# A slot-attention and FP8 feed-forward kernel: first loads reordered, one group of transposes and three split steps moved

## The chip, the cores and the metric

The kernel runs on one core of a Trainium2 chip. The metric is the device time of one execution in microseconds, as the median of several runs. A core has five engines that each work through a queue of their own in order: PE (TensorE), DVE (VectorE), ACT (ScalarE), POOL (GpSimd) and SP, which here issues most of the DMAs.

## The reference

Four sequences of 512 tokens with 512 channels pass through one layer: a gated slot attention with 16 heads (64 key channels, 64 slots, 128 value channels), then a feed-forward block whose weights are rounded to FP8.

```python
x = x + attn(layernorm(x), Wq, Wk, Wv, Wg, Ws, Wo, g_norm_weight)
x = x + ffn(layernorm(x), gate_w, up_w, down_w, gate_scale, up_scale, down_scale)

# attn, per head:
s = clip(h @ Ws, -32, 32); z = cumlogsumexp(s)      # over time
g = exp(z_before - z);     p = exp(s - z)
hk = hk * g + k p^T;       ok = (q * scale) hk       # first recurrence
hv = hv * g + p v^T;       ov = softmax(ok) hv       # second recurrence
o  = ov * rsqrt(mean(ov^2) + eps) * g_norm_weight * silu(h @ Wg)
return o @ Wo
# ffn:
return ((silu((h @ q(gate_w)) * gate_scale) * (h @ q(up_w)) * up_scale) @ q(down_w)) * down_scale
```

## The kernel before, in words

**Units.** Heads are taken in pairs (8 groups `g`), and a unit is one pair of heads for one sequence `b`. Sequences 0 and 1 go through all groups first, then 2 and 3; unit 0 is (0, 0), unit 1 is (0, 1). A sequence has 4 blocks of 128 tokens (`NT`), and 512 channels are 4 chunks (`KC`).

**Order.** The scheduling is manual: every engine executes its instructions in the order in which the Python code issues them. `first_unit` writes out unit 0 by hand, and `attention` writes out every later unit. Steps that are not tied to a place wait in two lists: `steps` holds the transposes of a later sequence's norm blocks (`next_step()` takes one), and `work` holds VectorE and ScalarE steps, mostly the splitting of weights. `other(n)` takes n entries of `work`, without a number as many as `pace[0]` says (2 in unit 1); `piece()` takes entries until one of them was a full step; `need(key)` takes entries until none with that name is left.

**Split operands.** Products of 32-bit precision are made from three float32r products: an operand is split into a high part (ScalarE, times `UNDER`), a low part and a third part (VectorE). For a norm block, `transposes(n)` turns the block with four TensorE transposes into a PSUM bank and ScalarE writes the high part (L358); `parts(n)` has VectorE write the low and the third part (L368, L370). The low part is then multiplied by 1/`DELTA` in place on ScalarE (`scale_low`, L310), one block later than its split, and after the last block through an entry of `work` of its own. For a weight matrix, `load_matrix` puts an entry `high(0)` (named with a trailing `_`) and one `step(n)` for each 512 columns into `work`: a step has ScalarE write the next high half (L253) and VectorE the two other parts (L260, or L262 for Wq, and L265). After the last step, SP writes the split matrix to DRAM (L273); steps of Wo also call `fetch()` for the next raw weights (L210).

**Sequence 0** is different: its first products use the unsplit values (`xn_whole`, and raw weights), and its split follows later.

**PSUM.** `bank()` hands out three banks in turn (scores, transposes, states); a product that gets a bank must wait until the reader of its last content is done. Projections (`proj`) have three buffers, and so the first write into one waits for the reader of a former projection.

**The start.** SP's queue loads block 0 of sequence 0, the two halves of Wv for the first pair of groups (`raw_v`, 512 KB each), blocks 1 to 3, then raw Ws, Wk, Wq, sequence 1 and raw Wg; the latter lands in the place that the split Wo takes later (tag `w_o`). In the norm of sequence 0, VectorE measures a block (L339 to L341), POOL takes a power (L342), VectorE normalises (L346), TensorE transposes (L353), ScalarE copies (L356). The measuring of block n + 1 is issued ahead of the normalising of block n. The values of block 0 (`values(0)`, L565) come between the transposes of blocks 0 and 1.

**The tail of unit 0 and unit 1.** After the gates and the softmax come the weights' transposes (ps_w, then wT at L758), `weight_slot` (ps_b at L611, masked on VectorE at L615), `read_out` (ps_ov at L772 and L781), then unit 1 with `slots` (ps_s, eT), `keys` (with `running_sum`, the scan z at L677, in between), `queries`, the transposes ps_e and ps_kn, `values(0)`, `values(1)`.

Of the kernel before, what the change touches and what calls it, by code (L numbers as in the profile page):

```python
# [44 lines left out]
P = 128  # L45
# [4 lines left out]
def kernel(  # L50
# [18 lines left out]
    nc = tc.nc  # L69
# [7 lines left out]
    KC = D // P  # L77
# [32 lines left out]
    def bank(name, n=None):  # L110
        if n is None:
            n = turn[0]
            turn[0] = (n + 1) % 3
        if n in held:
            held.pop(n)()
        return ps1.tile([P, 512], F32, tag=f"bank{n}", name=name)
# [50 lines left out]
    def other(count=None):  # L167
        for _ in range(count or pace[0]):
            if work:
                work.pop(0)[1]()  # L170

    def piece():

        while work:
            name, run = work.pop(0)
            run()
            if not name.endswith("_") and run is not scale_low:
                break

    def need(key):  # L180

        while any(name == key for name, _ in work):
            other(1)
# [4 lines left out]
    for g in range(NG):  # L188
# [3 lines left out]
        for nm in names:  # L192
            n = g if nm != "v" else 0 if g == 0 else (g + 1) // 2
# [5 lines left out]
    def fetch():  # L199
        if to_fetch:  # L200
            nm, g, part, chunks = to_fetch.pop(0)
            src, width = MATRICES[nm]
            tag = f"raw{fetched[0] % 2}"
            fetched[0] += 1
            w = one.tile([P, RAW], F32, tag=tag, name=f"raw_{nm}_{g}_{part}")[:, : chunks * width]
            if nm == "o":
                rows = src[g * HV : (g + 1) * HV, :]
            else:
                rows = src[part * chunks * P : (part + 1) * chunks * P, g * width : (g + 1) * width]
            nc.sync.dma_start(  # L210
                w.rearrange("p (c n) -> p c n", c=chunks), rows.rearrange("(c p) n -> p c n", p=P)
            )
            raw.setdefault((nm, g), []).append(w)
# [72 lines left out]
    def turned():  # L286

        return bool(work) and work[0][0][:3] == "xs_"

    def next_step():  # L290
        if steps:
            steps.pop(0)()
# [21 lines left out]
    whole = []  # L314

    def layernorm(b, which, n_bank=None, first=None):
# [33 lines left out]
        def transposes(n):  # L350
            pt = bank(f"ps_xn{which}_{b}_{n}", n_bank).rearrange("p (c t) -> p c t", c=KC)
            for c in range(KC):
                nc.tensor.transpose(pt[:, c, :], xn[n][:, c * P : (c + 1) * P], ident)  # L353
            hi = dst[0][:, :, n * P : (n + 1) * P]
            if start:
                nc.scalar.copy(whole[0][:, :, n * P : (n + 1) * P], pt)  # L356
            elif which == 1:
                nc.scalar.mul(hi, pt, UNDER)  # L358
            else:
                nc.scalar.copy(hi, pt)  # L360
            pts[n] = pt
# [513 lines left out]
    def exp_and_log():  # L875
        nc.scalar.preload_act_table_set("natural_log_exp_and_others")

    def first_unit():


        X = Heads(0, 0)

        parts = layernorm(0, 1, first=lambda: X.values(0))
        for nm in "skqv":
            load_matrix(nm, 0, True)
        for item in [item for item in work if item[0] in ("s_", "k_", "q_")]:
            work.remove(item)
            item[1]()
        X.values(1)
        for _ in range(5):  # L890
            piece()
        transposing = layernorm(1, 1)
        work.extend(parts())
        load_matrix("g", 0, True)
        other(2)
        X.slots()
        other(2)
        X.keys(X.running_sum)
        other(2)
        X.queries(None)  # L900
        X.turn_e()
        X.turn_k()
        other(2)
        X.values(2)
        other(2)
        X.key_states()
        X.inverse()
        X.values(3)
        fetch()
        fetch()  # L910
        load_matrix("o", 0, True)
        other(1)
        transposing()
        next_step()
        other(2)
        X.query_key()
        next_step()
        other(3)
        X.gate_main(0)
        X.slot_scores()  # L920
        X.value_states()
        next_step()
        next_step()
        X.softmax()
        X.softmax_exp()
        other(1)
        X.gate_main(1)
        X.slot_weights()
        other(1)
        X.gate_silu(0)  # L930
        X.gate_silu(1)
        exp_and_log()
        X.weight_slot()
        X.softmax_sum()
        need("xs_0")
        piece()
        piece()
        X.read_out()
        return X

    def attention(g, b, before, load, gated):

        X = Heads(g, b)
        even = g % 2 == 0
        small = other if even or b > 1 or pace[0] > 1 else piece
        first = pace[0] > 1 and even and b == 1

        def early_step():  # L950

            if not any(name.endswith("_m") for name, _ in work):
                next_step()

        need(f"xs_{b}")
        need("s")
        X.slots()
        load("s")
        if not even:
            early_step()  # L960
        before.scale_output()
        need("k")

        def running_sum():
            before.scale_other()
            X.running_sum()
            if first:
                other(1)
            else:
                small()  # L970

        X.keys(running_sum)
        load("k")
        if not even:
            early_step()
        need("q")
        X.queries(other if even or turned() else None)
        load("q")
        X.turn_e()
        if even:  # L980
            X.turn_k()
            next_step()
            if turned():
                other(1)
            need("v")
            X.values(0)
            X.values(1)
            before.turn_output(0)
            before.high_output(0)
            before.turn_output(1)  # L990
            before.high_output(1)
            X.key_states()
            X.inverse()
            X.query_key()
            other()
            X.values(2)
            before.split_output(0)
            next_step()
            other()
            X.values(3)  # L1000
            other()
            next_step()
            before.split_output(1)
        else:
            before.turn_output(0)
            X.turn_k()
            before.turn_output(1)
            before.high_output(0)
            before.high_output(1)
            X.query_key()  # L1010
            X.key_states()
            before.split_output(0)
            before.split_output(1)
            X.inverse()
            if work and work[0][1] is scale_low:
                other(1)
            if work and work[0][0] == "o":
                other()
        need("g")
        X.gate_main(0)  # L1020
        before.low_output(0)
        before.low_output(1)
        X.gate_mixed(0)
        if even:
            other()
            next_step()
        elif work and work[0][0] == "o":
            other()
        X.gate_main(1)
        X.gate_mixed(1)  # L1030
        load("g")
        if even:
            load("v")
        gated()
        X.gate_silu(0)
        X.gate_silu(1)
        exp_and_log()
        X.slot_scores()
        X.value_states()
        X.softmax()  # L1040
        if not turned():
            small()
        need("o")
        before.project_output(0)
        X.softmax_exp()
        before.add_output(0)
        before.project_output(1)
        X.slot_weights()
        before.add_output(1)
        next_step()  # L1050
        before.project_output(2, True)
        before.add_output(2)
        small()
        before.project_output(3)
        load("o")
        X.weight_slot()
        before.add_output(3)
        X.softmax_sum()
        if even or b > 1 or steps:
            other()  # L1060
        next_step()
        if turned():
            other(1)
        X.read_out()
        return X
# [81 lines left out]
    with tc.manual_schedule(engines=EVERY):  # L1147
        blocks = x[0].rearrange("(n p) d -> p n d", p=P)
        x1[0] = two.tile([P, NT, D], F32, tag="v", name="x1_0")
        for n in range(NT):  # L1150
            nc.sync.dma_start(x1[0][:, n, :], blocks[:, n, :])
            if n == 0:
                fetch()
                fetch()
        exp_and_log()
        fetch_first()
# [155 lines left out]
```

## Time and profile before

| | |
|---|---|
| median of 3 runs | 1462.33 us (1461.22 to 1462.84) |
| the profiled execution | 1460.5 us, of which 1458.8 us are the span of its instructions |
| TensorE busy | 1433.3 us (98%) |
| VectorE busy | 1101.6 us (76%) |
| ScalarE busy | 713.1 us (49%) |
| mean granted TensorE clock | 0.999 |
| unit 0 | until about 55 us |
| unit 1 | from there to about 98 us |

Times in the profile count from the first instruction. In a line of the timeline the first number is the start and the second the length, both in us; the bracket at the end is the idle time of the engine just before, and what ended it. PE matmul records may stand for several products that follow each other; a 32-bit product has two records and a float32r product one.

### The profile page before, as it was taken

The page shows a single profiled execution, that of the slowest core. Times are in us where ns is not written, and L with a number is a line of the kernel's source. Part 1 is how long each engine was busy: PE and PEld are TensorE (multiplying, and loading weights), DVE is VectorE, ACT ScalarE, POOL GpSimd, SP SyncE. Part 2 cuts the span into 40 slices and gives each one's busy share as a digit, 9 for nine tenths or more (in the row PEclk, how much of TensorE's full clock was granted, in tenths as well). Part 3 has the DMA queues.
Part 4 walks back from the last instruction along what each step waited for, and adds up shares of the span by engine and source line. Part 5 has one row for each costly group of instructions (what it writes and reads, how often), then busy time and mean ns, then how long its engine had stood idle before and what let it go on. Part 6 is the DMA issues. An engine that isn't in the chain of part 4 may idle for free.

```text
span 1458.8 us, 23013 instructions
## 1 busy us (share of the span) xinstructions
PE 1433.3 (98%) x9067; PEld 1171.4 (80%) x9067; DVE 1101.6 (76%) x1966; ACT 713.1 (49%) x1214; POOL 197.7 (14%) x206
## 2 busy tenths in 40 slices
PE   8999999999999999999999999999999999999998
PEld 4788888888888887888888888888888888888886
DVE  7788768876887689878888888898888874445333
ACT  4665555655564556454544564456345643222221
POOL 2011111111111111211111111111112120000000
PEclk9999999999999999999999999999999999999999
DMA  8275456564656464456546654666455562101000
GB/s 335 108 207 174 138 151 174 174 217 130 174 173 208 110 231 123 138 159 188 164 111 187 202 173 96 194 202 174 123 181 174 148 178 29 58 0 59 0 29 29
DMA packets 80715, 212.52 MB, mean 146 GB/s; under 512 B 6152, under 2 KB 34848, under 8 KB 75424
## 3 DMA queue, kind: packets, MB, share of 16 engines
q1 hardware_dynamic: 62080, 177.49, 32.8%
q0 software_dynamic: 18528, 33.58, 15.9%
q8 instruction: 71, 1.16, 0.3%
q14 instruction: 36, 0.29, 0.1%
HBM read 107.23 MB, written 108.00 MB: 148 GB/s over the span
## 4 chain that ended last, share of the span: by engine, by line
PE 82%; DVE 11%; issue 4%; ACT 2%; DMA 0%; POOL 0%; SPq 0%; DVEq 0%; ACTq 0%; POOLq 0%
PE ps_o L857 8%; PE ps_g L517 7%; PE ps_v L576 7%; PE ps_fg L1073 6%; PE ps_fu L1073 6%; PE ps_o_m L857 4%; PE ps_g_m L540 4%; PE ps_v_m L576 4%; PE ps_ov L781 4%; PE ps_s L517 3%; PE ps_q L517 3%; PE ps_k L517 3%; PE ps_fd L1122 3%; PE ps_fe L1122 2%; PE ps_b L611 2%
## 5 line engine op out<-in xcount | busy, mean ns | idle before, releaser
L873 POOL DMA_DIRECT2D stream<-y x128 | 112.9, 890 | 826.8 <-DVE y L872 819.7
L857 PE MATMUL ps_o<-w_o,oT 128*128 128x512 f32 x512 | 144.1, 403 | 0.0
L517 PE MATMUL ps_g<-xs,w_g 128*128 128x512 f32 x496 | 125.2, 394 | 0.0
L576 PE MATMUL ps_v<-w_v,xs 128*128 128x512 f32 x480 | 122.4, 397 | 0.3 <-ACT v L584 0.3
L1094 DVE SCALAR_TENSOR_TENSOR h<-ps_fu,scol,act 128x512 f32<-128x512 f32 x48 | 36.0, 750 | 105.9 <-PE ps_fu L1073 104.6
L867 ACT ACTIVATE y<-ps_o 128x512 f32<-128x512 f32 x128 | 76.6, 599 | 76.2 <-PE ps_o L857 73.4
L517 PEld LDWEIGHTS ps_g<-xs,w_g 128*128 128x128 f32 x496 | 91.7, 188 | 19.8
L857 PEld LDWEIGHTS ps_o<-w_o,oT 128*128 128x128 f32 x512 | 91.5, 188 | 16.8
L576 PEld LDWEIGHTS ps_v<-w_v,xs 128*128 128x128 f32 x480 | 87.7, 188 | 19.6 <-ACT v L584 0.8
L1073 PE MATMUL ps_fg<-xs,wf 128*128 128x512 f32 x384 | 96.5, 393 | 0.0
L1073 PE MATMUL ps_fu<-xs,wf 128*128 128x512 f32 x384 | 95.0, 389 | 0.0
L872 DVE TENSOR_TENSOR y<-y,ps_o_m 128x512 f32<-128x512 f32 x128 | 87.1, 680 | 9.7 <-ACT y L867 8.9
L584 ACT ACTIVATE v<-ps_v 128x512 f32<-128x512 f32 x60 | 36.0, 599 | 99.5 <-PE ps_v L576 99.5
L1073 PEld LDWEIGHTS ps_fu<-xs,wf 128*128 128x128 f32 x384 | 72.1, 188 | 15.2
L791 ACT ACTIVATE og<-ps_ov 128x512 f32<-128x512 f32 x64 | 38.1, 597 | 93.4 <-PE ps_ov L781 93.4
L1073 PEld LDWEIGHTS ps_fg<-xs,wf 128*128 128x128 f32 x384 | 71.1, 188 | 14.4
L585 DVE TENSOR_TENSOR v<-v,ps_v_m 128x512 f32<-128x512 f32 x60 | 41.0, 684 | 53.7 <-PE ps_v_m L576 53.7
L857 PE MATMUL ps_o_m<-w_o,oT 128*128 128x512 f32 x256 | 79.2, 391 | 0.1
L1100 ACT CAST both<-h 128x512 fp32r<-128x512 f32 x48 | 29.8, 621 | 96.8 <-DVE h L1094 96.8
L522 ACT ACTIVATE sg<-ps_g 128x512 f32<-128x512 f32 x62 | 37.2, 599 | 72.7 <-PE ps_g L517 58.0
L1091 ACT ACTIVATE act<-ps_fg,scol 128x512 f32<-128x512 f32 x48 | 33.0, 688 | 80.9 <-PE ps_fg L1073 80.9
L796 POOL TENSOR_TENSOR rs<-rs,mhalf 128x8 f32<-128x8 f32 x32 | 58.8, 1839 | 89.7 <-DVE rs L793 76.4
(169 smaller groups left out, 3260.8 us busy)
## 6 DMA issues: line engine op xcount, KB each, us to landing
stream<-y POOLq DMA_DIRECT2D x128, 256.0 KB, 5.9
split_v<-w_v SPq DMA_DIRECT2D x4, 3072.0 KB, 14.6
split_g<-w_g SPq DMA_DIRECT2D x8, 1536.0 KB, 6.8
split_o<-w_o SPq DMA_DIRECT2D x8, 1536.0 KB, 6.2
w_v<-split_v SPq DMA_DIRECT2D x4, 3072.0 KB, 15.4
w_g<-split_g SPq DMA_DIRECT2D x8, 1536.0 KB, 6.5
w_o<-split_o SPq DMA_DIRECT2D x8, 1536.0 KB, 9.4
rounded<-qw SPq DMA_DIRECT2D x36, 256.0 KB, 3.4
```

Source lines behind the costliest of these rows:

```text
L517: nc.tensor.matmul(self.p, products(self.nm, c, self.col0, i), xs[self.b][i][:, c, :], start=(i == 0 and c == 0), stop=(i == 1 and c == KC ...
L540: nc.tensor.matmul(self.m, products(self.nm, c, self.col0, 2), xs[self.b][2][:, c, :], start=(c == 0), stop=(c == KC - 1),)
L576: nc.tensor.matmul(dst, xs[b][i][:, c, n * P : (n + 1) * P], wt["v"][:, i, c * 2 * HV : (c + 1) * 2 * HV], start=(i == which[0] and c == 0 ...
L585: nc.vector.tensor_tensor(to, to, m, ALU.subtract)
L781: nc.tensor.matmul(po[h][:, n, :], self.bb[h][:, n, :], both_v[self.b][:, n, self.v0 + h * DV : self.v0 + (h + 1) * DV], start=False, stop ...
L796: nc.gpsimd.tensor_tensor(rs, rs, mhalf.rearrange("p (h n) -> p h n", h=HG), ALU.pow)
L857: nc.tensor.matmul(dst, self.oT[:, i, h, n * P : (n + 1) * P], wt["o"][:, i, h * D : (h + 1) * D], start=(i == which[0] and h == 0), stop= ...
L867: nc.scalar.mul(y, p, 1.0 + DELTA)
L872: nc.vector.tensor_tensor(y, y, m, ALU.subtract)
L873: nc.gpsimd.dma_start(stream[self.b][n * P : (n + 1) * P, :], y, accum_op=ALU.add)
L1073: nc.tensor.matmul(pp, w[:, c * P : (c + 1) * P], xs[b][k][:, c, :], start=(c == 0 and k == 0), stop=(c == KC - 1 and k == 1),)
L1122: nc.tensor.matmul(sums[n], parts[k][:, n * P : (n + 1) * P], fw[c][2], start=(c == 0 and k == 0), stop=(c == NFC - 1 and k == 1),)
```

## The change

Four edits:

1. SP's queue issues block 1 of sequence 0 between the two halves of Wv, not behind both.
2. ScalarE's copy of the transposed block 0 is two copies of half the chunks each. The first products of `values(0)` read the first half alone.
3. In `first_unit` the transposes of the last norm block of sequence 1 move from ahead of the softmax (`ps_okn`) to between `slot_weights` and the gates' Silu, that is ahead of `weight_slot` (`ps_b`). Its parts, which `other(1)` issued there, are issued by `need("xs_1")` after `weight_slot`. One of the two `piece()` calls goes, so that the second split step of Wg stays in `work`.
4. In unit 1, `running_sum` takes no entry of `work`; `queries` takes three (the Wg step, the first high half of Wo, the first Wo step); one more is taken between `values(0)` and `values(1)` (the second Wo step, with its fetch of raw Wk and its write to DRAM).

```diff
             if start:
-                nc.scalar.copy(whole[0][:, :, n * P : (n + 1) * P], pt)
+                for half in (0, 1) if n == 0 else (None,):
+                    cs = slice(None) if half is None else slice(half * KC // 2, (half + 1) * KC // 2)
+                    nc.scalar.copy(whole[0][:, cs, n * P : (n + 1) * P], pt[:, cs])
...
         X.value_states()
         next_step()
-        next_step()
         X.softmax()
         X.softmax_exp()
         other(1)
         X.gate_main(1)
         X.slot_weights()
-        other(1)
+        next_step()
         X.gate_silu(0)
         X.gate_silu(1)
         exp_and_log()
         X.weight_slot()
+        need("xs_1")
         X.softmax_sum()
         need("xs_0")
-        piece()
         piece()
         X.read_out()
...
             X.running_sum()
-            if first:
-                other(1)
-            else:
+            if not first:
                 small()
...
-        X.queries(other if even or turned() else None)
+        X.queries((lambda: other(3)) if first else other if even or turned() else None)
...
             X.values(0)
+            if first:
+                other(1)
             X.values(1)
...
             nc.sync.dma_start(x1[0][:, n, :], blocks[:, n, :])
-            if n == 0:
-                fetch()
+            if n < 2:
                 fetch()
```

In the order of the instructions, three things follow on ScalarE. The scaling of the third block's low part of sequence 1 (L310) moves from ahead of the two table loads of the Silu to behind them, next to the scaling of the fourth. The high part of the fourth block comes after the second gate's copy. The first high half of Wo goes behind the copy of qT, and waits for VectorE's second Wg step. VectorE masks ps_b ahead of the split of the fourth block, and takes the second Wg step and both Wo steps later. The banks of all later products are one further on in their turn, and the second values product of unit 1 gets the buffer of the queries' third product, whose reader is VectorE's subtraction for qT. From there on the order is the same on all engines.

## The prediction

> **What bounds the kernel now.** I read the page first, then the table by stretches for the stages that the diff touches, then TensorE's waits and the timelines of those stages.
>
> ```profile
> PE 1433.3 (98%) x9067; PEld 1171.4 (80%) x9067; DVE 1101.6 (76%) x1966; ACT 713.1 (49%) x1214; POOL 197.7 (14%) x206
> ```
>
> The stretches:
>
> ```profile
> 0.00:7.40 7.40, 3.92 (x19) 3.29 (x19) 1.58 (x4) 1.87 (x2) 3.47 (x13) 1.00 0.71 231
> 7.40:14.10 6.70, 5.53 (x21) 2.79 (x22) 4.38 (x12) 1.76 (x3) 2.15 (x3) 1.00 1.09 354
> 14.10:44.00 29.90, 29.90 (x138) 15.32 (x138) 26.84 (x51) 16.78 (x31) 3.81 (x4) 1.00 0.73 295
> 44.00:55.30 11.30, 10.02 (x78) 7.10 (x74) 8.25 (x16) 7.53 (x11) 0.00 (x0) 1.00 0.01 1
> 55.30:72.00 16.70, 16.33 (x78) 12.76 (x80) 12.18 (x21) 9.70 (x21) 1.65 (x1) 1.00 0.42 171
> ```
>
> TensorE is busy for 98% of the span, so only its idle time can be won. The second column of the stretches is the length and the third TensorE's busy time: 1.17 us are idle from 7.4 to 14.1, none to 44, 1.28 to 55.3, 0.37 to 72. The granted clock is 1.00 everywhere, so no speed is at stake. With what the timeline names, nearly all of this idle time can be placed:
>
> ```profile
> 8.48 0.69 DVE L339 BATCH_NORM_STATS2 stats<-x 128x6 f32<-128x512 f32 x1 [2.48 <-DMA x<-_attn_hidden_states_dram]
> 9.49 0.68 DVE L339 BATCH_NORM_STATS2 stats<-x 128x6 f32<-128x512 f32 x1
> 12.58 0.66 PE L353 MATMUL ps_xn<-ident,xn 128*128 128x128 f32 x4 [0.83 <-DVE xn L346]
> 13.57 0.66 PE L353 MATMUL ps_xn<-ident,xn 128*128 128x128 f32 x4 [0.33 <-DVE xn L346]
> 45.84 0.63 PE L593 MATMUL ps_okn<-ident,okT 128*128 128x128 f32 x4 [0.39 <-DVE sv L638]
> 51.13 1.16 PE L611 MATMUL ps_b<-wT,eT 64*128 64x128 f32 x16 [0.78 <-DVE wT L758]
> 53.54 1.28 ACT L876 ACT_TABLE_LOAD   x1
> 54.84 0.63 ACT L310 ACTIVATE xs<-xs 128x512 fp32r<-128x512 f32 x1
> 55.22 2.14 PE L517 MATMUL ps_s<-xs,w_s 128*128 128x512 f32 x8
> 60.90 2.11 PE L517 MATMUL ps_q<-xs,w_q 128*128 128x512 f32 x8
> 68.11 2.11 PE L576 MATMUL ps_v<-w_v,xs 128*128 128x512 f32 x8 [0.34 <-ACT v L584]
> ```
>
> Each bracket is what TensorE (or VectorE) stood still for just before. After 72 us its named waits add up to some 6 us over the whole rest. From the second values product of unit 1 on, the order is the same on all engines, so what is won or lost up to 72 us is carried to the end as it is.
>
> **A. The first 14 us.** The queue now issues block 1 before the second half of Wv. The landings (issue start plus time to landing) are 5.85 for Wv's first half, 7.8 for its second, 8.46 for block 1, about 9.1 for block 2 (2.74 plus 6.4) and 9.9 for block 3. They come in order of issue. So block 1 should land between 5.85 plus 0.65 (the spacing of blocks 1 and 2) and plus half of the 1.95 that 512 KB of Wv took: 6.5 to 6.9. Wv's second half takes its place at about 8.5. Nothing lands sooner for block 2, as the same bytes lie ahead of it. VectorE's queue holds block 2's statistics ahead of the normalisation of block 1; they now start at 9.15 instead of 9.49. The rest of that chain (statistics, POOL's power, normalisation up to block 3 at 13.51) was gapless behind that point but for POOL, so it all moves by 0.34, and TensorE's transposes of block 3 move from 13.57 to 13.23: **0.33 us**. From 14.1 to 44 all engines follow TensorE's events, so it is kept. Bounds: 0 if block 2 lands at 9.5 after all, 1.16 if both waits (0.83, 0.33) vanish.
>
> The halved copy lets values(0) start some 0.25 earlier (0.59 for 512 columns; an estimate for half from the 0.36 to 0.39 that a 128-column ScalarE copy takes at L807). TensorE then waits for xn of block 2 (ready 12.2) anyway: nothing gained, and ScalarE's extra instruction lies in its idle time. The same wait covers Wv: its second half is first read four records of 0.43 after the start, at 8.8, 0.3 after it lands; if it came up to 1 us later, the wait for block 2 would still hide it.
>
> **B. The tail of unit 0.** Taken in times of the profile of before. TensorE's transposes ps_xn_1_3 leave the place ahead of ps_okn. ps_okn waited until 45.84 because its PSUM bank was the one that ps_sv left, which VectorE was reading until 45.70; now it takes the next bank in turn, which ps_xn_1_1 left long before. Its only release is okT (VectorE, ends 44.85): it starts at 44.95, 0.89 earlier. Gate 1 (46.31) starts at 45.42, ps_w (49.74) at 48.85; the exponential between them (VectorE 45.72 to 47.13, ScalarE to 47.8) fits. wT then ends at 50.18 instead of 51.07, and the transposes (0.6) fill the time in which TensorE stood waiting for it. ps_b starts at 50.24 instead of 51.13: **0.89 us**. ps_b's products are masked before the split of block 3, which now follows them on VectorE, so read_out is not held, and ps_s of unit 1 can start at 54.31 instead of 55.22.
>
> What is late next is ScalarE. The copy of block 3's transposes ends about 50.55; behind it stand table load (1.28), two Silu (1.15), table load (1.28), and both scalings of the low parts, where before one of them had run ahead of the loads (at 50.43). Two back to back take 1.15 (the pair at 52.37), so they end at 55.47, as late as before. ps_s needs them for its fifth of eight products, which TensorE reaches at 54.31 + 0.99 = 55.30. It waits until 55.53: 0.23, and a group that starts after a wait is longer by 0.13 (2.11 against the 1.98 of ps_k). B is worth 0.91 - 0.36 = **0.55**. Bounds: 0.91 (no wait), and no gain at all if ScalarE is 0.55 later.
>
> The Trainium skill has a rule that speaks against just this edit. "ScalarE: Activation LUTs", in What ACT_TABLE_LOAD costs, puts each switch at about 1.28 us of load and 1.38 us of drain. By it, the two scalings behind two switches would come 2.76 later and B would be a loss of about 2.2. The trace does not show a drain: the load at 53.54 ends at 54.82, and the scaling starts at 54.84. I go by the trace.
>
> **C. Unit 1.** The second split step of Wg (VectorE, 1.40 for its two instructions, 57.36 to 58.76) leaves the front, where the row sums, the sum rs, eT and the scan queue behind it. ScalarE's part there does not move: og ends near 57.5, eT's copy near 58.0. VectorE's eT subtraction moves from 60.17 to about 58.9, the scan's end from 63.74 to 62.45 (held now by POOL's power, 1.65, and og), kT's end to 63.1. TensorE is ahead by 0.55 here. Two things go. ps_q started at 60.90, 0.05 behind eT's subtraction, and by the spacing of the products was due at 60.84: 0.06, and the 0.13 of a restart. The second values product waited 0.34 for ScalarE's copy of v, which queued behind rzT, qT, two Wo halves, e and kn; with the scan 1.3 earlier that copy ends near 66.8, while TensorE comes at 67.77 - 0.74 = 67.03: 0.34, and 0.13 of restart. Sum **0.66**.
>
> The moved steps put new things in the way. Wo's tile lies where raw Wg was, so ScalarE's first Wo half now waits for the Wg step's first instruction (VectorE 63.1 to 63.75); it comes at 64.2 anyway, 0.45 of cover, and behind it queue e, kn and v's copy, for which TensorE would wait. VectorE does Wg, then Wo, then qT's subtraction, ending near 66.9; in the new order the bank of that subtraction's operand is the one that the second values product needs. It comes at 67.03: cover 0.1, and past that every tenth is lost one to one. The second Wo step (1.4) falls into VectorE's idle time before 71.2 (1.67 us). Its DMAs and its fetch are on SP's queue: Wg's store goes from 58.83 to about 64.5, raw_k from 67.67 to about 68.5, Wo's store behind it. raw_k took 3.0 to land, so it is there at 71.5, and ScalarE first reads it after 74; the stores have no reader before the next pair of units. Free; with that cover gone, each would cost ScalarE a wait of its own length. From C I take half of the 0.1 that may be lost: 0.6. Bounds: 0.66 with another 0.13, and 0 if the qT wait is 0.7 long.
>
> **Sum.** 0.33 + 0.55 + 0.6 = 1.5 us. The profiled execution took 1460.5 (span 1458.8), 1.8 under the median of the three runs, 1462.33. It becomes 1459.0; the median, 1460.8. About 0.2% (2.9 us) is what a measurement of this kernel can tell from no change, so most of this forecast lies within it.
>
> **Rivals.**
> - *All covered waits go.* A at its bound 1.16, B 0.91, C 0.79, and the 0.4 for e (ps_oT, named once after 60 us) too: 3.3 us, 1459.0 for the median, just over 0.2%. For it: every one of these waits is named in the profile. Against: block 2's bytes come no sooner.
> - *ScalarE becomes the bound at the unit's border.* If the two scalings end at 57.0 or later instead of 55.47, ps_s's wait (1.5 more) eats A, B and C: that is where it turns. A stop of a load's own length (1.28) behind each of the two loads would bring 2.56, and the sum is 1.5 - 2.56, thus 1.1 slower, 1463.4. Against: the 0.02 between load and next instruction. A late split of block 3 on VectorE (ends 54.1, needed at 54.3) works through the same queue, with 0.2 of cover. By the drain that the Trainium skill states under ScalarE: Activation LUTs, it would be 1463.6.
> - *Nothing at the start, and unit 1 gives back.* If block 2 lands as late as it was used and qT's wait is 0.7, only B's 0.5 stays: 1461.8.
>
> **How the numbers follow.** The forecast (0.7 to 2.6 us won) has 0.54, the full relief 0.27, the weak case 0.11, ScalarE's bound 0.08. Faster by over 0.2% takes the full relief's share, nearly whole, and a little of the forecast's upper end: 0.28. Slower by over 0.2% needs ScalarE's bound with more than one drain's length and unit 1's loss together, or a mechanism that I don't see: 0.06. Within: 0.66. The range goes from the full relief less the 0.6 by which runs lie off their median (1458.4) to the weak case plus 1.1, which takes in part of ScalarE's bound (1462.9).
>
> **What would show it.** In the changed profile: block 1's statistics before 7 and block 2's at 9.1 to 9.2; the last block's transposes at 13.2; ps_okn without a wait, ps_b about 1.2 earlier than 51.13 with a wait of 0.3 for wT; a wait of ps_s, 0.2 long, for the scalings (L310); no wait of the second values product for v. Wrong would be: a ps_s wait over 0.5, a values wait for qT over 0.3, statistics of block 2 at 9.5, or any new wait after 72 us.

## The result and the profile after

The changed kernel took 1459.68 us (median of 22 runs, 1459.27 to 1460.85), the kernel before 1462.22 (22 runs, 1461.12 to 1463.82). The ratio is 0.9986, 95% interval 0.9980 to 0.9991: 2.5 us faster, between 1.3 and 2.9. A second comparison (below) gave 1.7. The forecast was 1.5 us faster (1460.8), with a range of 1458.4 to 1462.9.

The profiled execution of after took 1459.7, of which 1458.0 are its span. That is only 0.8 less than the 1460.5 of the execution shown for before, although the medians differ by 2.5. The profiled execution of before was quicker than every one of the 22 runs; that of after sits on its median. The page and the stretches of after, with the same columns as before:

```profile
PE 1434.8 (98%) x9067; PEld 1172.4 (80%) x9067; DVE 1102.4 (76%) x1966; ACT 713.1 (49%) x1215; POOL 197.8 (14%) x206
```

```profile
0.00:7.40 7.40, 4.43 (x19) 3.63 (x19) 1.58 (x4) 1.77 (x3) 3.48 (x13) 1.00 0.71 203
7.40:14.10 6.70, 6.37 (x18) 3.10 (x19) 4.48 (x12) 1.66 (x4) 2.14 (x3) 1.00 1.08 348
44.00:55.30 11.30, 10.85 (x88) 7.90 (x84) 8.61 (x16) 7.31 (x11) 0.00 (x0) 1.00 0.01 1
55.30:72.00 16.70, 16.53 (x95) 13.19 (x95) 13.19 (x22) 10.30 (x22) 1.65 (x1) 1.00 0.38 150
```

TensorE's idle time falls from 1.28 to 0.45 in the unit 0 tail and from 0.37 to 0.17 in unit 1. From 7.4 to 14.1 it falls from 1.17 to 0.33, but that is no gain: the same products took longer. TensorE's timeline of after shows it, and the answers to the other steps:

```profile
7.33 5.23 PE L567 MATMUL ps_v<-raw_v,xn_whole 128*128 128x512 f32 x8 [0.46 <-ACT xn_whole L358]
...
13.93 0.66 PE L353 MATMUL ps_xn<-ident,xn 128*128 128x128 f32 x4 [0.33 <-DVE xn L346]
...
45.27 0.66 PE L595 MATMUL ps_okn<-ident,okT 128*128 128x128 f32 x4
50.58 1.16 PE L613 MATMUL ps_b<-wT,eT 64*128 64x128 f32 x16 [0.35 <-DVE wT L760]
54.67 2.37 PE L519 MATMUL ps_s<-xs,w_s 128*128 128x512 f32 x8
60.51 1.98 PE L519 MATMUL ps_q<-xs,w_q 128*128 128x512 f32 x8
67.18 2.11 PE L578 MATMUL ps_v<-w_v,xs 128*128 128x512 f32 x8 [0.17 <-DVE qT L546]
```

The first values product took 5.23 us where it took 3.70 before. The last norm block came at 13.93, later than before (13.57). VectorE's timeline says why:

```profile
7.76 0.69 DVE L339 BATCH_NORM_STATS2 stats<-x 128x6 f32<-128x512 f32 x1 [2.05 <-DMA x<-_attn_hidden_states_dram]
9.84 0.69 DVE L339 BATCH_NORM_STATS2 stats<-x 128x6 f32<-128x512 f32 x1 [0.99 <-DMA x<-_attn_hidden_states_dram]
```

Block 1 is there at 7.76, and then VectorE waits 0.99 for block 2, which lands at 9.84 and not at 9.1. So in this one pair of executions the start lost 0.36 and the tail with unit 1 won 1.29: the values product that ended its wait at 68.11 starts at 67.18, 0.93 earlier. That shift then stays between 0.8 and 0.96 to the last unit.

### The profile page after: what moved, and what is told of

Same layout as the page of the kernel before. It is cut to its first block, busy times and chain, and to the rows that moved or that the text cites. A ratio compares the mean times of both kernels' runs of the same rounds, so it can differ in the third digit from the quotient of the medians.

```text
span 1458.0 us, 23015 instructions
## 1 busy us (share of the span) xinstructions
PE 1434.8 (98%) x9067; PEld 1172.4 (80%) x9067; DVE 1102.4 (76%) x1966; ACT 713.1 (49%) x1215; POOL 197.8 (14%) x206
## 4 chain that ended last, share of the span: by engine, by line
PE 83%; DVE 11%; issue 3%; ACT 2%; DMA 0%; POOL 0%; SPq 0%; DVEq 0%; POOLq 0%
PE ps_o L859 8%; PE ps_g L519 8%; PE ps_v L578 8%; PE ps_fg L1074 6%; PE ps_fu L1074 6%; PE ps_o_m L859 4%; PE ps_g_m L542 4%; PE ps_v_m L578 4%; PE ps_ov L783 4%; PE ps_s L519 3%; PE ps_q L519 3%; PE ps_k L519 3%; PE ps_fd L1123 3%; PE ps_fe L1123 2%; PE ps_b L613 2%
```

## The experiments

All were run beside the kernel before on the same chip; a single kernel's ratio is uncertain by about 0.1%. The stages were therefore also read from the traces, where they repeat to 0.05 us. In the table (us, one execution each, from the timelines) "gap" is the time from block 2's statistics to the second values product of unit 0, and "units 0-1" the time from that product to ps_oT in unit 1.

| kernel | statistics of block 1, 2 | first values product, length | second values product | gap | units 0-1 |
|---|---|---|---|---|---|
| before | 8.48, 9.49 | 3.70 | 14.06 | 4.57 | 56.91 |
| after | 7.76, 9.84 | 5.23 | 14.42 | 4.58 | 55.62 |
| start_only | 6.98, 9.32 | 5.40 | 13.96 | 4.64 | 56.91 |
| tail_only | 8.67, 9.69 | 5.19 | 14.41 | 4.72 | 56.91 |
| unit1_only | 9.15, 10.17 | 5.36 | 14.73 | 4.56 | 55.80 |
| tail_unit1 | 9.19, 10.20 | 3.70 | 14.77 | 4.57 | 55.64 |
| whole_again | 6.85, 9.32 | 6.23 | 15.43 | 6.11 | 55.62 |
| scale_early | 6.83, 9.56 | 4.76 | 14.14 | 4.58 | 55.23 |
| blocks_first | 7.70, 8.71 | 6.11 | 15.35 | 6.64 | 55.63 |
| warm_20 | 6.98, 9.46 | 3.70 | 14.03 | 4.57 | 55.63 |
| before_warm | 9.29, 10.31 | 3.70 | 14.88 | 4.57 | 56.95 |
| start_warm | 6.84, 9.10 | 3.70 | 13.68 | 4.58 | 56.90 |
| scale_warm | 7.29, 10.03 | 4.22 with a wait | 14.60 | 4.57 | 55.25 |
| scale_warm_blocks | 7.04, 8.05 | 3.99 | 12.95 | 4.90 | 55.24 |

**The parts alone.** First, the loads and the halved copy:

```diff
-            if n == 0:
-                fetch()
+            if n < 2:
                 fetch()
...
-                nc.scalar.copy(whole[0][:, :, n * P : (n + 1) * P], pt)
+                for half in (0, 1) if n == 0 else (None,):
...
```

> Only edits 1 and 2 (order of the first loads, first copy in halves). Theory S (the start is worth more than forecast, because the traced execution of before had an unusually early block 1 and the usual one starts later): 1.0 to 1.6 us faster than before in the median, and block 1's statistics are well ahead of block 2's in the trace. Theory T (the tail and unit 1 are worth more than the two traces show, the start nothing): within 0.4 us of before.

Measured: 1461.10 (before 1461.62), ratio 0.9998 (0.9989 to 1.0007). The medians differ by 0.52, between the two theories (S asked for at least 1.0, T for at most 0.4), and that is not resolved from nothing. In the trace block 1's statistics are well ahead of block 2's (6.98 and 9.32), as theory S expected.

Second, the norm block's transposes:

```diff
         X.value_states()
         next_step()
-        next_step()
...
         X.slot_weights()
-        other(1)
+        next_step()
...
         X.weight_slot()
+        need("xs_1")
```

> Only edit 3 without the removed piece (norm block's transposes ahead of ps_b, its parts behind weight_slot; both Wg steps stay in front of unit 1). Both theories expect ps_b 0.9 earlier against the start of unit 0's second values, and a wait of ps_s for the two scalings of some 0.3 us. Theory S: 0.4 to 0.7 us faster in the median. Theory T: 1.2 or more.

Measured: 1462.15 (before 1461.62), ratio 1.0003 (0.9995 to 1.0012): nothing. Both theories' times were wrong, and the trace gives the reason. TensorE's and VectorE's timelines of tail_only:

```profile
54.66 2.37 PE L517 MATMUL ps_s<-xs,w_s 128*128 128x512 f32 x8
...
61.21 2.11 PE L517 MATMUL ps_q<-xs,w_q 128*128 128x512 f32 x8 [0.54 <-DVE eT L544]
...
68.42 2.14 PE L576 MATMUL ps_v<-w_v,xs 128*128 128x512 f32 x8 [0.32 <-ACT v L584]
```

```profile
57.66 0.68 DVE L260 TENSOR_TENSOR w_g<-raw_g,w_g 128x512 fp32r<-128x512 f32 x1
58.38 0.69 DVE L265 SCALAR_TENSOR_TENSOR w_g<-w_g 128x512 fp32r<-128x512 f32 x1
58.99 1.27 DVE L792 TENSOR_REDUCE rs<-og 128x4 f32<-128x512 f32 x2
60.30 0.17 DVE L793 SCALAR_TENSOR_TENSOR rs<-rs,sm 128x8 f32<-128x8 f32 x1
60.38 0.18 DVE L150 COPY scol<-ps_scol 128x25 f32<-128x25 f32 x1
60.47 0.68 DVE L544 TENSOR_TENSOR eT<-eT,ps_s_m 128x512 f32<-128x512 f32 x1
```

The lines of before that belong beside them, and ScalarE's timeline of tail_only:

```profile
55.38 1.14 ACT L253 ACTIVATE w_g<-raw_g 128x512 fp32r<-128x512 f32 x2
60.17 0.68 DVE L544 TENSOR_TENSOR eT<-eT,ps_s_m 128x512 f32<-128x512 f32 x1
```

```profile
53.33 1.28 ACT L876 ACT_TABLE_LOAD   x1
54.62 1.15 ACT L310 ACTIVATE xs<-xs 128x512 fp32r<-128x512 f32 x2
55.68 1.14 ACT L253 ACTIVATE w_g<-raw_g 128x512 fp32r<-128x512 f32 x2
```

All times here are compared from the second values product on (14.41 in tail_only, 14.06 in before). ps_s comes 0.91 sooner (40.25 against 41.16). ScalarE's second table load comes 0.56 sooner (38.92 against 39.48), but two scalings stand behind it instead of one, and so its next instruction, the high half of Wg, comes only 0.05 sooner (41.27 against 41.32). VectorE waits for that half, then goes through the two Wg steps and the row sums without a gap, and reaches the eT subtraction 0.05 sooner (46.06 against 46.11). ps_q, which needs it, now waits 0.54, and the whole 0.91 is given back by ps_oT (16.66 from ps_s, against 15.75).

Third, unit 1's order on the old tail:

```diff
         need("xs_0")
         piece()
-        piece()
...
-            if first:
-                other(1)
-            else:
+            if not first:
                 small()
...
-        X.queries(other if even or turned() else None)
+        X.queries((lambda: other(3)) if first else other if even or turned() else None)
...
             X.values(0)
+            if first:
+                other(1)
             X.values(1)
```

> Only edit 4 and the removed piece (second Wg step and both Wo steps later in unit 1), before's tail of unit 0. Theory S: the waits of ps_q and of the second values product go: 0.4 to 0.7 us faster. Theory T: 1 or more. A third possibility, that it only pays together with the tail, gives 0 to 0.3 here.

Measured: 1460.88 (before 1461.62), ratio 0.9995 (0.9986 to 1.0004); by the trace 1.11 (56.91 to 55.80). The medians' 0.74 is not resolved; the trace shows more than theory S's 0.7 and does not fit the third possibility. Its timeline has no wait at all at ps_q and at the second values product:

```profile
61.48 1.98 PE L517 MATMUL ps_q<-xs,w_q 128*128 128x512 f32 x8
...
67.81 1.98 PE L576 MATMUL ps_v<-w_v,xs 128*128 128x512 f32 x8
```

> Edits 3 and 4 together with the old start. Theory S: 1.2 to 1.4 us faster (the 1.29 by which unit 1's second values product came nearer to the first values in the two traces), so about 1.2 short of the whole change. Theory T: 2.2 or more, as good as the whole change.

This kernel has both edits above and the old start. Measured: 1460.80 (before 1461.62), ratio 0.9992 (0.9983 to 1.0002); by the trace 1.27. So the two are not a sum: 0.00 alone, 1.11 alone, 1.27 together. Unit 1's order pays almost all, and the tail adds 0.16 once that order has made room. The median falls 0.4 short of theory S's 1.2, within its interval; nothing speaks for theory T.

**The whole again, and what paces it.**

> The whole change once more, beside the kernel before on this chip. Theory P (the parts: start 0.3, tail and unit 1 together 1.27 by the traces, nothing else): 1.3 to 1.9 us faster than before. Theory M (the whole is more than its parts, since something happens only when all four edits are in): 2.3 or more again. Block 2's statistics are expected anywhere from 9.1 to 9.9; from there to the second values product 4.6, in both theories.

Measured: 1459.86 (before 1461.56), ratio 0.9989 (0.9980 to 0.9998), 1.7 faster: theory P. The interval (0.3 to 2.9 us) does not exclude theory M, but units 0-1 took 55.62, as in after and as in tail_unit1 (55.64), so nothing new happens there when all four edits are in. Both theories missed the gap, which was 6.11 and not 4.6: the start was the slowest of all.

```profile
7.56 6.23 PE L567 MATMUL ps_v<-raw_v,xn_whole 128*128 128x512 f32 x8 [0.46 <-ACT xn_whole L358]
13.63 1.04 PE L353 MATMUL ps_xn<-ident,xn 128*128 128x128 f32 x8
```

One line more, which scales the third block's low part before the table loads:

```diff
         X.slot_weights()
+        scale_low()
         next_step()
         X.gate_silu(0)
```

> The whole change, with the scaling of the third block's low part issued just ahead of the last norm block's transposes, so that one scaling instead of two stands behind the table loads. Theory Q (ScalarE's queue behind the second table load paces the border of the units, as the give-back of the tail alone says): ps_s loses its wait (0.23 to 0.37), and og, eT and what hangs on them come 0.3 earlier, so that the wait for qT (0.17) goes too: 0.4 to 0.7 us faster than the whole change. Rival (VectorE's order paces it, ScalarE's share is slack): 0 to 0.25.

Measured: 1459.39 (whole change on the same chip 1459.86, a difference that is not resolved), by the trace 0.39 less in units 0-1 (55.23 against 55.62). ScalarE's timeline of after, then of scale_early:

```profile
53.35 1.28 ACT L878 ACT_TABLE_LOAD   x1
54.64 1.15 ACT L310 ACTIVATE xs<-xs 128x512 fp32r<-128x512 f32 x2
55.70 1.14 ACT L253 ACTIVATE w_g<-raw_g 128x512 fp32r<-128x512 f32 x2
```

```profile
53.20 1.28 ACT L878 ACT_TABLE_LOAD   x1
54.49 0.63 ACT L310 ACTIVATE xs<-xs 128x512 fp32r<-128x512 f32 x1
55.03 1.14 ACT L253 ACTIVATE w_g<-raw_g 128x512 fp32r<-128x512 f32 x2
```

From the end of the load to the start of w_g, 0.55 instead of 1.07. ps_s then took 2.14 instead of 2.37, and the second values product is no longer listed with a wait for qT (0.17). By the traces that is theory Q, at its lower end. A part of that wait is left, though: the product starts 1.08 behind the start of ps_v_m, where unit1_only has 0.91 and after 1.24.

**The start.** Two loads ahead of Wv's second half:

```diff
-            if n < 2:
+            if n in (0, 2):
                 fetch()
```

> The whole change, with blocks 1 and 2 both ahead of Wv's second half. Theory R (block 2's landing gates the first 14 us through its statistics, which stand ahead of block 1's normalisation): block 2's statistics at 8.3 to 9.0, the second values product 0.4 to 0.9 earlier. Rival (Wv's second half becomes the gate): the first values product waits for it past 9.5, ends after 12, and the second one is as late as in the whole change or later.

Measured: 1459.31 (1457.83 to 1460.87), the widest spread of the kernels run beside it. Block 2's statistics came at 8.71, as theory R has it, but the second values product at 15.35, as late as the rival has it, and not for the rival's reason: the first product took 6.11 without a stop. Wv's second half landed at 10.1 (issued at 2.70, 7.4 to landing), and the slow product came to its second half only after that (its fifth weight load of eight is at 10.32). So this trace does not settle what the order of loads is worth.

Next, a longer warm-up (transposes whose result nobody reads, which TensorE runs until the first block is there):

```diff
-    WARM = 14
+    WARM = 20
```

> The whole change with 20 warm-up transposes instead of 14, which fill TensorE's idle time up to the first block's own transposes. Theory H (in part of the executions the granted clock is half until about 10.5, which makes the first values product 5.2 long instead of 3.7, and that reaches the end): the first values product is 3.7 in the trace, and the median falls by 0.3 to 0.8 with less spread. Rival (the length of that product is hidden by the chain of block 2): within 0.2 of the whole change.

Measured: 1459.35 (1459.03 to 1460.33), against 1459.86 (1458.92 to 1460.62) for the whole change. The first product was 3.70 long. The median moved as theory H says, but a difference of 0.5 between 11 runs each is not resolved.

> The kernel before with 20 warm-up transposes instead of 14. Theory H (the time at which the clock gate grants full speed, 5.5 to 12.7 us in the traces so far, makes the first values product 3.7 to 6.2 long and is what spreads the executions): that product is 3.7 here, the spread is below that of before, and the median 0.3 to 0.9 below it. Rival: same median within 0.2, same spread.

Measured: 1461.30 (before 1462.12), ratio 0.9994 (0.9986 to 1.0003); spread 1.8 in 11 runs against 3.0 in 29. The product is 3.70 long; the gain is not resolved either.

> Edits 1 and 2 on top of the 20 warm-up transposes, so that the first loads and the halved copy are seen without the clock. Forecast of the prediction for part A: 0.33 us faster than before_warm, with block 2's statistics at about 9.2 and the second values product 4.6 to 4.9 behind them. Rival 1 (both waits vanish): 1.0 or more. Rival 2 (the loads' landing differs between executions by more than the order moves it, so that nothing is left): within 0.15.

Measured: 1460.77, 0.53 under before_warm, which lies between the forecast and rival 1, and is not resolved. VectorE's timelines of before_warm and of start_warm:

```profile
9.29 0.69 DVE L339 BATCH_NORM_STATS2 stats<-x 128x6 f32<-128x512 f32 x1 [3.40 <-DMA x<-_attn_hidden_states_dram]
10.31 0.68 DVE L339 BATCH_NORM_STATS2 stats<-x 128x6 f32<-128x512 f32 x1
```

```profile
6.84 0.69 DVE L339 BATCH_NORM_STATS2 stats<-x 128x6 f32<-128x512 f32 x1 [0.88 <-DMA x<-_attn_hidden_states_dram]
9.10 0.70 DVE L339 BATCH_NORM_STATS2 stats<-x 128x6 f32<-128x512 f32 x1 [1.16 <-DMA x<-_attn_hidden_states_dram]
```

In the old order block 1 is the gate: block 2's statistics follow 1.01 or 1.02 behind in all five traces, without a wait. In the new order (seven traces, those with two blocks ahead left out) block 2 is the gate, behind a wait.

These two join the edits already shown: early scaling with the warm-up, then also two blocks first.

> The whole change with the early scaling and 20 warm-up transposes. If both gains are independent (0.4 by the traces for the scaling, 0.3 to 0.6 for the clock): 2.4 to 3.2 us faster than before in the median, and faster than either alone. If the scaling's gain is lost at the next wait: no better than 1.9.

Measured: 1459.20 (before 1462.12), ratio 0.9981 (0.9972 to 0.9990), 2.9 us faster, as expected if both gains add; that it beats either alone (1459.39 and 1459.35, on another chip) is not resolved. In its trace Wv's second half was late: the first product stood still for 0.29 until 9.43, and the wait for block 2 hid it.

> The same with blocks 1 and 2 ahead of Wv's second half. Theory R with the clock at full speed: block 2's statistics at 8.4 to 8.9, and the second values product is then set by block 3 (statistics at 10.9 in the trace with the old warm-up): 0 to 0.3 earlier than in the kernel without this order. Rival (Wv's second half gates): later by up to 0.5.

Measured: 1457.92 (7 runs, 1457.36 to 1458.19), ratio 0.9972 (0.9961 to 0.9983): 4.2 us faster than before, and the fastest kernel here, though its interval overlaps that of scale_warm. The second values product came at 12.95, earlier than in any other trace and 1.65 earlier than in scale_warm, which is more than either theory expected. It is set by block 3, as theory R has it: 3.12 from block 3's statistics to it, against 3.11 in before. But block 3's statistics came at 9.83 here, not at 10.86. Wv's second half was late here too (issued at 2.70, 6.4 to landing; the first product is 0.29 longer than 3.70), and the wait for block 3 hid it.

## Why the prediction was right, and where not

**Direction and mechanism hold.** The wait of ps_okn went, ps_b came 0.91 sooner after the second values product, ps_s waited for the scalings by 0.23 (2.21 from its start to that of ps_s_m, against 1.98), and no new wait stood after 72 us. Tail and unit 1 together were forecast at 1.15 and measured at 1.27 and 1.29.

**B and C are right as terms of the whole, not as the worth of each edit.** In the whole change the stretch up to ps_s_m won 0.91 - 0.23 = 0.68, where 0.55 was forecast: the 0.13 booked for a restart did not come on top of ps_s's wait. The rest of unit 1 won 0.61, where 0.6 was forecast. But alone the edits are worth 0.00 and 1.11. The prediction priced the tail with unit 1's new order in place and did not say that the tail's gain hangs on it: it asked what was late next at ps_s, and found ScalarE's 0.23, but not what was late after that if unit 1 kept its order (ps_q's wait of 0.54 for eT).

Within C, two errors cancel, so that its number is partly luck. ps_q's gain came as forecast (0.18, forecast 0.06 and 0.13). ps_kn and the product behind it came 0.25 sooner after ps_e, since the wait for kT is gone (ps_kn 0.63 behind ps_e before, 0.43 after); the prediction did not count that. The second values product, in turn, won 0.17 where 0.34 and 0.13 were forecast: it no longer waits for v, but 0.17 for qT. VectorE's line in after:

```profile
66.45 0.68 DVE L546 TENSOR_TENSOR qT<-qT,ps_q_m 128x512 f32<-128x512 f32 x1
```

Less the 0.36 by which this execution started later, it ends at 66.77, close to the forecast 66.9. TensorE was the one that came sooner than forecast, at about 66.5 instead of 67.03, by what had not been counted at ps_s and ps_kn. So the cover, put at 0.1, was negative.

**A: the step holds, its size is not resolved.** In the profiled pair the start lost 0.36, and block 2's statistics at 9.84 lie past the 9.5 that the prediction had named as a sign of being wrong. The prediction noted that the profiled execution was 1.8 under the median, and still took its landings as usual: block 1's statistics came at 8.48 there, and at 8.67 to 9.29 in the other four traces of the old order. What the edit takes away, however, is the time between block 2's landing and its statistics, and this varies little. In the five traces of the old order block 2 landed at 9.1 to 9.9 (issue plus time to landing), each time 0.3 to 0.5 ahead of its statistics; in the new order the statistics start as it lands. So the forecast 0.33 is about what the order is worth as long as block 2 itself lands no sooner and no later, and its landings in the two orders overlap (9.1 to 9.9, and 9.1 to 10.0). Compared over all executions, block 2's statistics have their median at 10.17 in the five traces of the old order and at 9.46 in the seven of the new one, 0.71 apart, but their means are only 0.45 apart: what goes beyond 0.3 to 0.5 can be scatter of the landings. With about 4.57 from there to the second values product in nearly every trace, the start is worth 0.3 to 0.7, and with the 1.29 that makes 1.6 to 2.0, which lies in both measured intervals, as the forecast 1.5 does. Why the first comparison gave 2.5 stays open. By time the start alone was never resolved (0.52 against before, 0.53 against before_warm). The halved copy cut TensorE's wait for it from 0.68 to 0.46, by 0.22 where 0.25 was estimated; that it brings nothing further on was not tried alone.

**"No speed is at stake" was wrong.** It held for the execution that it was read from, not for others. The first values product was 3.7 to 6.2 long in the fourteen traces. The stretches of start_only show the clock for once:

```profile
5.00:8.50 3.50, 2.24 (x7) 1.25 (x8) 1.57 (x4) 0.65 (x2) 0.50 (x2) 0.89 1.01 320
8.50:12.00 3.50, 3.50 (x6) 1.34 (x5) 2.55 (x8) 0.00 (x0) 1.03 (x3) 0.62 1.13 328
```

The last three columns are granted clock, DMA share and GB/s: 0.62 while that product ran. In the other traces the column shows 1.00 even where the product is long, and the spacing of its weight loads tells instead. In before, then in after:

```profile
8.35 0.19 PEld L565 LDWEIGHTS ps_v<-raw_v,xn_whole 128*128 128x128 f32 x1 [0.24 <-issue]
8.78 0.19 PEld L565 LDWEIGHTS ps_v<-raw_v,xn_whole 128*128 128x128 f32 x1 [0.24 <-issue]
```

```profile
8.35 0.33 PEld L567 LDWEIGHTS ps_v<-raw_v,xn_whole 128*128 128x128 f32 x1 [0.52 <-issue]
9.20 0.33 PEld L567 LDWEIGHTS ps_v<-raw_v,xn_whole 128*128 128x128 f32 x1 [0.52 <-issue]
10.06 0.33 PEld L567 LDWEIGHTS ps_v<-raw_v,xn_whole 128*128 128x128 f32 x1 [0.52 <-issue]
10.68 0.19 PEld L567 LDWEIGHTS ps_v<-raw_v,xn_whole 128*128 128x128 f32 x1 [0.29 <-issue]
```

That is one every 0.43 us against one every 0.85 us, until after reaches 0.43 as well (10.68, then 11.11). The Trainium skill, TensorE: Matmul & The Clock Gate, Part 1, says that the array runs at half speed until it has been busy through one free-running window of about 3.4 us. The traces agree as far as they go: six more warm-up transposes left no product over 4.3 in five of five, against two of nine without. In start_only the clock was not late but fell back: the first block's four transposes took 0.66 at 5.79, as in before (1.11 in after), and 0.50 was granted from 8.0 to 11.0.

Of the nine traces with 14 warm-up transposes, two of the four in the old order of loads have a long product, and all five with the changed start. These are too few to tell whether the changed start has a part in it. At lengths up to 5.4 the chain of block 2 hides it but for 0.15 (gap 4.56 to 4.72); at 6.23 it costs 1.5 (gap 6.11).

**No stop behind a table load.** In after the first instruction behind the second table load came 0.01 behind its end (53.35 + 1.28, 54.64), and the load itself 0.02 behind the Silu. The rival built on a stop there had no part in it, but ScalarE's queue was indeed the next bound: scale_early.

## What to carry to other kernels

Before a gain at one wait is booked, follow the engine that then arrives early to its next two waits, in the order that will stand there: here 0.91 us won in one unit was worth nothing until the next unit's order made room. Edits that feed one queue are tested together and apart, since neither 0.00 nor 1.11 gives the 1.27. One trace of a start that hangs on loads says little about when they land: here the landings moved by 0.8 from one execution to the next, while the distance that the edit takes away stayed at 0.3 to 0.5. Read that distance in several executions, and compare stages in the traces when the medians can't resolve them.

## What the runs showed that was not expected

- The same first loads, issued in the same order, land differently from one execution to the next: block 1 at 8.48 to 9.29 in the old order, block 2 at 9.10 to 10.03 in the new one.
- The first values product took 3.7 to 6.2 us, by how long the clock stayed at half, and the profile's clock column showed it in one trace of fourteen.
- With the clock at full speed and two blocks ahead of Wv's second half, the second values product came 1.1 us earlier than in the best trace of the old order (12.95 against 14.06). That is one execution, and block 3 landed early in it.
